# Two-layer spectral and cosine convolution on one core: the row sums of layer 1 are issued one step later

## The chip, the cores and the metric

The kernel runs on one core of a Trainium2 chip. The metric is the device time of one execution in microseconds (us). Five engines work side by side, each through a queue of its own, in order: PE (matrix multiplications; PEld is its weight load), DVE (VectorE), ACT (ScalarE), POOL (GpSimd) and SP, which here only issues DMAs. An engine whose next instruction waits for another engine does nothing else meanwhile.

## The reference

The input `x` is 4 images of 512 x 512 pixels with 16 channels, in float32. Each of two layers adds a convolution of the group-normalised input to the input. Layer 0 is a long convolution in the frequency domain; its code is left out here, since the change is in layer 1:

```python
def _L1_conv_ref(x, kernel, bias, radius):
    ones_f = jnp.ones((K, K, C, 1), dtype=x.dtype)          # K = 3, C = 16
    input_norm = jnp.sqrt(lax.conv_general_dilated(x * x, ones_f, strides, 'SAME', dimension_numbers=DN) + EPS)
    kernel_norm = jnp.sqrt(jnp.sum(kernel * kernel, axis=(0, 1, 2), keepdims=True) + EPS)
    y = lax.conv_general_dilated(x, kernel / kernel_norm, strides, 'SAME', dimension_numbers=DN)
    y = y / input_norm
    y = 1.0 - jnp.arccos(y) * (2.0 / jnp.pi)
    y = y * (jnp.tanh(kernel_norm / radius) * jnp.tanh(input_norm / radius))
    return y + bias
...
x = x + _L0_conv_ref(_gn(x), L0_conv_h0, L0_conv_numerators, L0_conv_denumerator)
x = x + _L1_conv_ref(_gn(x), L1_conv_kernel, L1_conv_bias, L1_conv_radius)
```

So every output pixel needs, beside its 3 x 3 convolution, the sum of squares of the 3 x 3 x 16 inputs around it, of which the kernel takes the root, the reciprocal and the hyperbolic tangent.

## The kernel before

The kernel has four phases, one after the other: the filter of layer 0, the forward transform, the product in the frequency domain, and `last_phase`, which transforms back (until about 14,740 us in the profile) and then computes layer 1. Only layer 1, the last 1,750 us, is touched.

**Units and groups.** Layer 1 cuts the four images into 64 groups; a group is 32 columns of one image over all its 512 rows. A group `g` has four units `u = 4g ... 4g+3`, each of 128 rows x 32 columns x 16 channels, and also four blocks `q = 4g ... 4g+3`, each of 8 columns over all rows. For a unit or a block there are these pieces of work (the lines are those of the profile):

- `block(q)`: PE transposes the input (`pt`, L1183), ACT normalises it (`xn`, L1191) and squares it (`x2`, L1193).
- `squares(q)`: PE sums the squares over channels (four matmuls, `p2`, L1209, into a PSUM tile of one buffer), DVE copies the sums to `e_sum` (L1213). The sums of a group need one column of each neighbour, which POOL copies: at `k == 0` into the group before (L1215), at `k == 3` into the group after (L1218).
- `over_w(g)`: POOL adds the three neighbouring columns (two additions, L1222 and L1223, into `e_sum3`; the profile calls it `e_sum`).
- `norms(g)`: PE adds the three neighbouring rows (three matmuls into `pn`, L1230 to L1232), ACT takes the root (`l_inn`, L1237) and, once for two groups, in the odd one, the tanh (`l_th`, L1239), DVE the reciprocal (`l_rin`, L1241). It issues no DMA.
- `border(g)`: POOL gathers the columns beside a group (L1259), PE transposes them (L1262), DVE normalises them (`e_bn`, three instructions, L1271).
- `conv(u)`: PE, twelve matmuls of the 3 x 3 convolution (L1279) and one of the border (L1287), into one of four PSUM tiles `pc`.
- `cosine(u)`: DVE, `pc` times `l_rin` (`e_y`, L1297). `root` and `factors`: seven instructions of ACT (L1303 to L1315). `gate` and `signed`: two of POOL (L1320, L1325), the first of which reads `l_th`. `chain(u)`: DVE, three products (L1331), one more (L1332), and `e_o` (L1334), after which the tile `pc` is free again. `finish(u)`: POOL adds the input (L1339), SP stores the result (L1341).

Beside that, `prepare()` makes the next image ready until about 15,760 us: POOL adds (`p_x`, L1071), DVE takes statistics (L1067), SP loads and stores.

**What sets the order.** A loop calls `step(u)`, and `step` calls the pieces above, each for a unit or group ahead of or behind `u` (`lead` is 14). In `step` the sums of group `g` and the norms of group `g` come from two lines:

```python
g, k = divmod(u + lead - 3 - 4, 4)
if k == 0 and 0 <= g < n_groups:
    norms(g)
...
g, k = divmod(u + lead - 2 - 4, 4)
if k == 0 and 0 <= g < n_groups:
    over_w(g)
```

The first lies near the start of `step`, before `block` and `conv`; the second at its end. So `over_w(g)` is issued at the end of step `4g-8`, and `norms(g)` near the start of the next one, `4g-7`, just after `squares(4g+6)`. The order in which the instructions then stand in the queues is not this order of calls: a scheduler of the framework places each instruction on its engine, from the order of the calls, the dependencies and the buffers. A change of one call can therefore move other instructions too, on every engine.

Of the kernel before, what the change touches and what calls it, by code (L numbers as in the profile page):

```python
# [961 lines left out]
def last_phase(tc, cst, x, y_d, yw_d, t_d, kern, bias, radius, out):  # L962
    nc = tc.nc
    with ExitStack() as ctx:
# [206 lines left out]
        def load(g):  # L1171
            t = xp.tile([P, 4, 32, C], F32, name="xt")
            b, wt, w = order[g // 16], g % 16 // 4, g % 4 * 32
            nc.sync.dma_start(
                out=t, in_=t_d[b][wt].rearrange("(h p) w c -> p h w c", p=P)[:, :, w : w + 32, :]
            )
            xt[g] = t

        def block(q):

            pt = ps_t.tile([P, N], F32, name="pt")
            for h in range(4):
                nc.tensor.transpose(  # L1183
                    pt[:, h * P : (h + 1) * P],
                    xt[q // 4][:, h, q % 4 * 8 : q % 4 * 8 + 8, :].rearrange("p w c -> p (w c)"),
                    ident,
                )
            xn = np_.tile([P, N + 2], F32, name="xn")
            nc.gpsimd.memset(xn[:, 0 : N + 2 : N + 1], 0.0)
            vec = vecs[order[q // 64]]  # L1190
            nc.scalar.activation(xn[:, 1 : N + 1], pt, AF.Identity, scale=vec[:, 0:1], bias=vec[:, 1:2])  # L1191
            x2 = ew.tile([P, N], F32, name="x2")
            nc.scalar.activation(x2, xn[:, 1 : N + 1], AF.Square)  # L1193
            xns[q], x2s[q] = xn, x2
# [9 lines left out]
        def squares(q):  # L1204

            g, k = q // 4, q % 4
            p2 = ps_s.tile([P, 4, 8], F32, name="p2", tag="gn_ps")
            for h in range(4):
                nc.tensor.matmul(p2[:, h], x2s[q][:, h * P : (h + 1) * P], cols, start=True, stop=True)  # L1209
            del x2s[q]  # L1210
            if g not in sums:
                edges(g)
            nc.vector.tensor_copy(sums[g][:, :, 1 + 8 * k : 9 + 8 * k], p2)  # L1213
            if k == 0 and g % 16 > 0:
                nc.gpsimd.tensor_copy(sums[g - 1][:, :, 33:34], sums[g][:, :, 1:2])  # L1215
            if k == 3 and g % 16 < 15:
                edges(g + 1)
                nc.gpsimd.tensor_copy(sums[g + 1][:, :, 0:1], sums[g][:, :, 32:33])  # L1218
# [7 lines left out]
        def norms(g):  # L1226

            s3 = st["s3"]
            pn = ps_n.tile([P, 4, 32], F32, name="pn")
            nc.tensor.matmul(pn, over_h[:, 0], s3, start=True, stop=False)  # L1230
            nc.tensor.matmul(pn[:, 1:4], over_h[:, 1], s3[:, 0:3], start=False, stop=False)
            nc.tensor.matmul(pn[:, 0:3], over_h[:, 2], s3[:, 1:4], start=False, stop=True)  # L1232
            if g % 2 == 0:
                st["inn"] = ew.tile([P, 2, 4, 32], F32, name="l_inn")
                st["th"] = ew.tile([P, 2, 4, 32], F32, name="l_th", bufs=4)
            inn, th = st["inn"], st["th"]
            nc.scalar.activation(inn[:, g % 2], pn, AF.Sqrt, bias=eps1)  # L1237
            if g % 2:
                nc.scalar.activation(th, inn, AF.Tanh, scale=rrad)  # L1239
            rin = ew.tile([P, 4, 32], F32, name="l_rin", bufs=4)  # L1240
            nc.vector.reciprocal(rin, inn[:, g % 2])  # L1241
            rins[g], ths[g] = rin, th[:, g % 2]
# [9 lines left out]
        def border(g):  # L1252

            t = ew.tile([P, 4, 3, 2, C], F32, name="e_bx")
            for side in range(2):
                at, w = (g + 2 * side - 1, 31 - 31 * side)
                if at // 16 != g // 16 or at < 0:
                    at, w = g, 0
                nc.gpsimd.tensor_copy(t[:, :, :, side], bc(xt[at][:, :, w, :], 2, [P, 4, 3, C]))  # L1259
            pt = ps_t.tile([P, N], F32, name="pt")  # L1260
            for h in range(4):
                nc.tensor.transpose(pt[:96, h * P : (h + 1) * P],  # L1262
                                    t[:, h].rearrange("p d s c -> p (d s c)"), ident)
            bx = ew.tile([96, N], F32, name="e_bn")
            nc.gpsimd.memset(bx[0:32, 0:1], 0.0)
            nc.gpsimd.memset(bx[64:96, N - 1 : N], 0.0)
            vec = vecs[order[g // 16]]
            for dh in range(3):
                r = slice(32 * dh, 32 * dh + 32)
                lo, hi = max(1 - dh, 0), min(N + 1 - dh, N)  # L1270
                nc.vector.tensor_scalar(bx[r, lo:hi], pt[r, lo + dh - 1 : hi + dh - 1],  # L1271
                                        vec[r, 0:1], vec[r, 1:2], ALU.mult, ALU.add)
            borders[g] = bx

        def conv(u):
            h, ts = u % 4, list(terms(u // 4))
            pc = ps_c.tile(sh, F32, name="pc")
            for n, (q, dh, lo, hi, o) in enumerate(ts):
                nc.tensor.matmul(  # L1279
                    pc[:, lo:hi, :].rearrange("p w j -> p (w j)"),  # L1280
                    xns[q][:, h * P + dh : h * P + dh + P],
                    bands[dh][:, o : o + hi - lo, :].rearrange("p w j -> p (w j)"),
                    start=(n == 0), stop=False,
                )

            lo, hi = int(u // 4 % 16 == 0), 2 - int(u // 4 % 16 == 15)
            nc.tensor.matmul(  # L1287
                pc[:, 31 * lo : 31 * hi - 30 : 31, :],
                borders[u // 4][:, h * P : (h + 1) * P], eband[:, lo:hi], start=False, stop=True,
            )  # L1290
            if h == 3:
                del borders[u // 4]
            pcs[u] = pc

        def cosine(u):
            y = ew.tile(sh, F32, name="e_y", bufs=4)
            nc.vector.tensor_mul(y, pcs[u], bc(rins[u // 4][:, u % 4, :], 2, sh))  # L1297
            st["y", u] = y

        def root(u):  # L1300

            v = ew.tile(sh, F32, name="e_v", bufs=3)
            nc.scalar.activation(v, st["y", u], AF.Abs)  # L1303
            nc.scalar.activation(v, v, AF.Relu, scale=-1.0, bias=1.0)
            nc.scalar.activation(pcs[u], v, AF.Sqrt, scale=ARC[7] ** 2)  # L1305
            st["v", u] = v
# [11 lines left out]
        def gate(u):  # L1318
            t = ew.tile(sh, F32, name="e_gate")
            nc.gpsimd.tensor_mul(t, bc(ths[u // 4][:, u % 4, :], 2, sh), bc(ktn, 1, sh))  # L1320
            st["gate", u] = t

        def signed(u):
            t = st["gate", u]
            nc.gpsimd.tensor_mul(t, t, st.pop(("y", u)))  # L1325
# [11 lines left out]
        def finish(u):  # L1337
            g, h, o = u // 4, u % 4, st.pop(("o", u))
            nc.gpsimd.tensor_add(o, o, xt[g][:, h])  # L1339
            w = g % 16 * 32  # L1340
            nc.sync.dma_start(out=out[order[g // 16], h * P : (h + 1) * P, w : w + 32, :], in_=o)  # L1341

        lead = 14

        def step(u):
            if u % 4 == 0 and (u + lead) // 4 + 2 < n_groups:
                load((u + lead) // 4 + 2)
            if 0 <= u + lead - 1 < n_units:
                squares(u + lead - 1)

            g, k = divmod(u + lead - 3 - 4, 4)
            if k == 0 and 0 <= g < n_groups:
                norms(g)
            if u + lead < n_units:
                block(u + lead)
            if u % 4 == 2 and 0 <= u + 6 < n_units:
                border((u + 6) // 4)
            if 0 <= u + 3 < n_units:
                conv(u + 3)
            if 0 <= u < n_units:  # L1360
                signed(u)
            if 0 <= u - 1 < n_units:
                finish(u - 1)
            if 0 <= u + 1 < n_units:
                root(u + 1)
                gate(u + 1)
                factors(u + 1)
            if 0 <= u < n_units:
                chain(u)
            if 0 <= u + 2 < n_units:  # L1370
                cosine(u + 2)
# [3 lines that stand above are left out]
            if u >= 0:  # L1375
                next(beside, None)
            for q in [q for q in xns if q < u]:
                del xns[q]
# [5 lines left out]
        for u in range(-lead, n_units + 1):  # L1384
            step(u)
# [50 lines left out]
```

## Time and profile before

| what | us |
|---|---|
| median of 3 runs | 16473.95 |
| lowest and highest of them | 16464.4 and 16498.5 |
| the profiled execution, its own time | 16489.29 |
| its span in the profile | 16487.4 |
| layer 1 within it (from about 14,740) | 1,750 |
| PE's waits for `over_w` within it (60 of the 64 groups) | 135.7 |

The profile comes from one execution, which lies 15 us above the median; 2 us of it lie outside the span. Lines of a timeline give the start, the duration, the engine, the line, the operation, what is written and read, and in square brackets how long the engine was idle before it and what ended the wait. A matmul of float32 data is shown as two records on PE, so the twelve of a `conv` are counted as 24; the four transposes of a `block` are counted as 4.

### The profile page before, as it was taken

To read this page: it belongs to the slowest core of one execution; us is meant where nothing else is said; L and a number is where in the kernel's file an instruction comes from. 1 tells how busy PE (TensorE), PEld (TensorE's weight loads), DVE (VectorE), ACT (ScalarE), POOL (GpSimd) and SP (SyncE) were. 2 spreads that over 40 slices of the span, in tenths; PEclk is the share of its full clock that TensorE was granted. 3 is DMA by queue.
4 is the path that set the end of the run, shared out by engine and by line. 5 is a ranking of instruction groups with operands and counts; after the bars stand their busy time and mean duration, and the time that the engine had idled before them with its cause. 6 is when DMAs were issued, how large, how long until landed. Compare 5 with 4: busy or idle time off the path is not lost. (4 is left out here: it accounts for less than half of the span.)

```text
span 16487.4 us, 538106 instructions
## 1 busy us (share of the span) xinstructions
PE 15039.9 (91%) x232588; PEld 11221.5 (68%) x232588; DVE 10549.6 (64%) x20763; ACT 8870.6 (54%) x17007; POOL 10203.4 (62%) x9645
## 2 busy tenths in 40 slices
PE   7999999999988889898988899888889998988898
PEld 5555555554567777677777777777777777777787
DVE  8999999974545555555555555555555552447877
ACT  4666666653345555555555555555555551027888
POOL 7777777763356666666666666666666660237766
PEclk8999999999999999999999999999999999989999
DMA  4888888888888888888888888888888886885531
GB/s 139 241 244 247 240 243 248 240 244 250 251 282 328 324 326 330 317 327 329 328 329 317 326 328 327 317 318 324 324 326 329 326 321 232 313 279 167 167 110 67
DMA packets 2914640, 4542.92 MB, mean 276 GB/s; under 512 B 126114, under 2 KB 2094460, under 8 KB 2801422
## 3 DMA queue, kind: packets, MB, share of 16 engines
q1 hardware_dynamic: 2703070, 3836.37, 67.9%
q0 software_dynamic: 172336, 605.00, 9.5%
q10 hardware_dynamic: 36864, 67.13, 1.2%
q8 instruction: 1833, 30.03, 0.7%
q14 instruction: 537, 4.40, 0.1%
HBM read 3030.71 MB, written 1477.31 MB: 273 GB/s over the span
## 5 line engine op out<-in xcount | busy, mean ns | idle before, releaser
L828 PE MATMUL pg<-c_dg,g 64*128 64x128 f32 x32832 | 2838.7, 290 | 344.4 <-ACT gh L728 192.2
L844 PE MATMUL pm<-xe,gh 128*32 128x64 f32 x131328 | 2380.2, 222 | 520.0 <-issue 299.3
L844 PEld LDWEIGHTS pm<-xe,gh 128*32 128x32 f32 x131328 | 2001.1, 110 | 1113.6 <-issue 891.7
L828 PEld LDWEIGHTS pg<-c_dg,g 64*128 64x128 f32 x32832 | 2277.5, 189 | 690.3 <-issue 248.1
L873 DVE TENSOR_TENSOR z<-zq,pz 128x256 f32<-128x256 f32 x2052 | 859.5, 419 | 2634.6 <-ACT zq L872 2567.4
L726 DVE COPY gh<-pg 128x512 f32<-128x512 f32 x2046 | 1408.2, 688 | 1208.9 <-PE pg L828 1205.8
L458 PE MATMUL pt<-ev_in,c_todd 128*128 128x512 f32 x4096 | 1927.5, 609 | 16.2 <-DMA ev_in<-g_d 16.2
L797 POOL TENSOR_TENSOR xu<-xe,c_late 128x256 f32<-128x256 f32 x2052 | 1391.7, 702 | 808.5 <-ACT xe L728 791.2
L388 DVE RECIPROCAL dn<-dn 128x256 f32<-128x256 f32 x1024 | 1722.8, 1724 | 17.6
L728 ACT COPY yf<-pm 128x512 f32<-128x512 f32 x2046 | 1211.4, 592 | 886.9 <-PE pm L844 873.2
L389 POOL TENSOR_TENSOR sp<-m,dn 128x512 f32<-128x512 f32 x1024 | 1300.9, 1271 | 592.4 <-DVE dn L388 552.0
L808 ACT COPY xe<-xl 64x1024 f32<-64x1024 f32 x513 | 538.7, 1050 | 1877.9 <-POOL xl L799 1877.8
L728 ACT COPY gh<-pg 128x512 f32<-128x512 f32 x2058 | 1200.2, 583 | 368.8 <-PE pg L828 365.7
L865 PE MATMUL pz<-c_ident,yf 128*128 128x128 f32 x8208 | 1371.7, 290 | 24.2 <-issue 10.8
L458 PEld LDWEIGHTS pt<-ev_in,c_todd 128*128 128x128 f32 x4096 | 728.2, 190 | 920.6 <-issue 792.3
L417 ACT COPY st<-pg 128x256 f32<-128x256 f32 x2048 | 616.8, 391 | 1301.5 <-PE pg L406 1301.3
L406 PEld LDWEIGHTS pg<-c_dinv,sp 64*128 64x128 f32 x16384 | 1005.5, 196 | 442.2 <-ACT sp L394 232.6
L799 POOL TENSOR_TENSOR xl<-xl,xu 128x1024 f32<-128x1024 f32 x513 | 1209.5, 2358 | 40.2
L406 PE MATMUL pg<-c_dinv,sp 64*128 64x128 f32 x16384 | 1108.2, 287 | 60.2 <-ACT sp L394 44.6
L881 POOL TENSOR_TENSOR zd<-z 128x512 f32<-128x512 f32 x513 | 653.7, 1274 | 765.4 <-DVE z L873 765.3
L1279 PE MATMUL pc<-l_band,xn 128*128 128x160 f32 (+2 forms) x6144 | 1076.2, 333 | 51.7 <-DVE e_o L1334 51.7
L913 POOL DMA_DIRECT2D y_d<-yo x511 | 296.5, 580 | 1325.0 <-ACT yo L728 1299.8
(211 smaller groups left out, 30193.2 us busy)
## 6 DMA issues: line engine op xcount, KB each, us to landing
xe<-xf_d SPq DMA_DIRECT2D x1026, 1536.0 KB
g<-g_d SPq DMA_DIRECT2D x511, 1024.0 KB
g_d<-st SPq DMA_DIRECT2D x256, 1024.0 KB
ev_in<-g_d SPq DMA_DIRECT2D x1024, 256.0 KB
g_d<-ot SPq DMA_DIRECT2D x1024, 256.0 KB
xf_d<-xe POOLq DMA_DIRECT2D x513, 448.0 KB, 8.2
xf_d<-xl POOLq DMA_DIRECT2D x513, 448.0 KB, 5.4
x_d<-xo SPq DMA_DIRECT2D x128, 1024.0 KB
```

What stands on the lines that cost most here:

```text
L388: nc.vector.reciprocal(dn, dn)
L389: nc.gpsimd.tensor_mul(w["sp"][:, v], w["m"][:, v], bc(dn, 2, [P, 2, 2, P]))
L406: nc.tensor.matmul(pg[u][:, n, k].rearrange("p a x -> p (a x)"), w["sp"][q, n, k, c, :], dinv[q, 2 * kp + k, c, :], start=(c == 0), stop=( ...
L458: nc.tensor.matmul(pt, todd[:, c, kc, hh * P : hh * P + P], ev[:, kc, c], start=(kc == 0), stop=(kc == 1),)
L726: nc.vector.tensor_copy(dst, src)
L728: nc.scalar.copy(dst, src)
L797: nc.gpsimd.tensor_mul(u[:, :, h, c], xe[:, :, h, 1 - c], bc(late[:, 1 + c], 2, [P, F, 2]))
L799: nc.gpsimd.tensor_add(xl.rearrange("p f h c k -> p (f h c k)"), xl.rearrange("p f h c k -> p (f h c k)"), u.rearrange("p f h c k -> p (f ...
L828: nc.tensor.matmul(pg[c][:, j % 4], g[half, j], dg[half], start=True, stop=True)
L844: nc.tensor.matmul(pm[32 * q : 32 * q + 32, g % 8], gh[:, f].rearrange("p c j -> p (c j)"), xe[:, :, f].rearrange("p t h c k -> p t (h c k ...
L865: nc.tensor.transpose(pz[:, t % 4].rearrange("p v q x -> p (v q x)"), y[:, at].rearrange("p g x -> p (g x)"), ident)
L1279: nc.tensor.matmul(pc[:, lo:hi, :].rearrange("p w j -> p (w j)"), xns[q][:, h * P + dh : h * P + dh + P], bands[dh][:, o : o + hi - lo, :] ...
```

## The change

`norms(g)` moves from step `4g-7` to step `4g-6`. Its place within the step, just after `squares` and before `block`, stays, and so does the place of `over_w(g)` at the end of step `4g-8`. Nothing is added or removed; the instructions and their operands are the same.

```diff
@@ -1348,7 +1348,7 @@
             if 0 <= u + lead - 1 < n_units:
                 squares(u + lead - 1)
 
-            g, k = divmod(u + lead - 3 - 4, 4)
+            g, k = divmod(u + lead - 8, 4)
             if k == 0 and 0 <= g < n_groups:
                 norms(g)
             if u + lead < n_units:
```

## The prediction

> **What bounds the kernel now.** I first cut layer 1 into stretches by the busy time of each engine. Here is one stretch while the next image is still prepared, and one after; the columns are PE, PEld, DVE, ACT, POOL and PE's granted clock.
>
> ```profile
> core 0: us, PE busy (x) PEld busy (x) DVE busy (x) ACT busy (x) POOL busy (x), PEclk, DMA share, GB/s
> 15100.00:15300.00 200.00, 171.97 (x1166) 151.49 (x1165) 165.87 (x334) 163.95 (x284) 149.28 (x183) 0.93 0.50 165
> ...
> 16100.00:16300.00 200.00, 180.87 (x1228) 159.60 (x1228) 151.77 (x249) 169.80 (x292) 125.83 (x183) 0.95 0.22 77
> ```
>
> PE leads with 86% and 90%, but ACT and DVE are close: whatever PE gains, they must be able to follow. DMA is half used. Next, who waits for whom, from 15,200 to 16,300 us (total, times, longest):
>
> ```profile
> PE pn L1230 <- POOL e_sum L1223: 78.5, 41, 7.9
> PE pc L1279 <- DVE e_o L1334: 31.9, 45, 3.0
> ACT l_inn L1237 <- PE pn L1232: 7.1, 3, 3.7
> POOL p_x L1071 <- DMA p_x<-in_x: 5.1, 4, 3.3
> ```
>
> Most of PE's idle time ends with `over_w`, on which the first norms matmul waits; in all of layer 1 it is 135.7 us in 60 groups. The second wait is for a free `pc`: a conv can start when DVE's `e_o` four units back is done. How the two look in time, after preparation has ended:
>
> ```profile
> 16202.21 1.04 PE L1209 MATMUL p<-c_cols,x 128*128 128x8 f32 x8
> 16204.15 3.98 PE L1279 MATMUL pc<-l_band,xn 128*128 128x512 f32 x24 [0.90 <-DVE e_o L1334]
> ...
> 16214.00 1.04 PE L1209 MATMUL p<-c_cols,x 128*128 128x8 f32 x8
> 16214.89 1.07 PE L1183 MATMUL pt<-c_ident,xt 128*128 128x128 f32 x8
> 16217.68 0.80 PE L1230 MATMUL pn<-e_sum,c_over_h 128*128 128x128 f32 x2 [1.72 <-POOL e_sum L1223]
> ```
>
> The norms come right behind the squares that they need (here with two blocks of transposes between), so PE sits out the chain copy (DVE) - copy (POOL) - two additions (POOL). A last look, while the image is prepared, at the longest kind:
>
> ```profile
> 14906.67 2.85 POOL L1071 TENSOR_TENSOR p_x<-p_x,p_y 128x1024 f32<-128x1024 f32 x1 [5.11 <-DMA p_x<-in_x]
> 14910.83 2.84 POOL L1071 TENSOR_TENSOR p_x<-p_x,p_y 128x1024 f32<-128x1024 f32 x1
> 14914.59 0.80 PE L1230 MATMUL pn<-e_sum,c_over_h 128*128 128x128 f32 x2 [9.84 <-POOL e_sum L1223]
> ```
>
> POOL, in order, waits for a load and works 2 x 2.85 us on the next image, with `over_w` behind it; PE waits 9.84 us.
>
> **What the Trainium skill says.** "Perfetto Trace Analysis", Optimization Strategy: a gap that repeats on the engine that should be saturated can mean too few SBUF or PSUM buffers. The 0.90 us gap is of that kind (four `pc` tiles); the 1.72 us one is a plain dependency. "TensorE: Matmul & The Clock Gate", What's actually happening: the PE clock is halved after an idle window of about 3.4 us, and the window runs free. The trace agrees in direction: a conv whose 24 matmuls take 3.82 us otherwise takes 4.2 to 6.0 after norms waits of over 2.5 us; after 1.5 to 1.7 us it is sometimes 3.7, sometimes 4.5 to 5.5. "ScalarE: Activation LUTs", What ACT_TABLE_LOAD costs: 1283 ns a load; the trace has 1283, and the built order still has one tanh per pair of groups, so I count no more loads.
>
> **The change part by part.** No instruction is added; I compare the built orders of both versions.
>
> *Norms on PE.* Only 22 of 64 groups get them later. Counted from a group's first block, five squares stood ahead of its norms before (its own four and the neighbour's one that it needs); now it is eight (groups 5, 7, 9, 11, 17, 19, 21, 23, 25, 29, 33), seven (35, 45, 49, 51, 53, 55, 57, 59, 61) or six (13, 41). They are all odd. The even groups keep their place directly behind the squares, so they keep their waits (1.3 to 1.6 us mostly). Taking the wait of each of the 22 from the timeline: 44.6 us in the eleven, 16.6 in the nine, 12.1 + 0.6 in the two: **-73.9 us**. In these groups the matmuls of the next conv took 13.7 us beyond 3.82 each: **-13.7 us**, if the waits caused it.
>
> *POOL.* Before those odd norms POOL has only come one `finish` further, PE two or three convs. So `over_w` is one to three units (about 6 us each) ahead; these waits go whole, the long ones too unless something else takes them up.
>
> *Root on ACT.* It now stands one unit (5.1 us of work) later, and in odd groups PE reaches its norms after conv `4g-4` rather than `4g-7`. ACT may stand idle for it: from the same block's transposes ACT works 5.1 us to the root, PE 6.3 (conv 3.9, squares 0.9, norms 0.75, rest), so about 1.3 us a pair of groups. ACT waits more than that for PE's transposes already (60.8 us from 15,960 to 16,400); I count zero. Behind the root wait the next block's normalising and squaring, which PE's squares need only after another conv. The tanh is one unit nearer its first `gate`, with two left; zero.
>
> *DVE, where the cost is.* The reciprocal (0.86 us pitch) moves one unit, and the scheduler repacked the queue around it. A conv needs, after the squares before it, DVE's `e_sum` copy, then what stands up to `e_o`. In the example above that is copy 0.1 + `e_o` 0.75 = 0.90 with nothing of PE's between, 0.42 with a border's transposes. Late (nine pairs, groups 44 to 61) the new queue has, once a pair, copy - L1332 - `e_y` - `e_o`, and once copy - L1332 - reciprocal - `e_o`. PE has one block's transposes (0.48) to cover it: 0.1 + 0.6 + 0.6 + 0.75 + 0.1 (from engine to engine) - 0.48 = 1.7, and with 0.86 for the reciprocal 1.9. That makes 3.6 a pair for 0.90 + 0.42 = 1.3 before: 9 x 2.3 = **+20.7 us**. Behind the waiting conv stand its squares and the next transposes, for which ACT then waits. While the image is prepared (15 pairs, 4 to 33) the copy is followed by L1332 and an `e_bn` (0.8), 1.8 us for 0.4, and the eight L1067 in a row (0.29 each) delay another `e_o` by some 0.6: 15 x 2.0 = **+30 us**, an estimate from these durations.
>
> *SP.* Norms move past no DMA, but loads and stores are repacked. POOL's waits for the load of `p_x` are 22.9 us in layer 1, in 10 times; bounds: that much less, or that much more. I take the middle, zero.
>
> Sum: -73.9 - 13.7 + 20.7 + 30 = **-36.9 us**, from the profiled 16489.3 to 16452.4; the median of the runs is 15.3 lower, so **16437**. Two runs of before differ by up to 34 us, so I take 0.2% (33 us) as what can be told from no change.
>
> **The rivals.**
>
> *The full gain* (part of faster). DVE uses its slack (17 to 24%) and no wait replaces the old one: -87.6, 16386. For it: DVE waits for squares often (70.5 us from 15,960 to 16,400). Against: those waits are what ties `e_o` to the squares.
>
> *It moves to `pc` and little is left* (same). Of the 73.9 us, 48.8 lie in six groups with waits over 4.9 us, where POOL stood behind a late load. The same POOL delay also holds `signed`, hence `e_o`, hence a conv; and now pairs of L1071 stand directly ahead of the copy for even groups. If half of it comes back: -36.9 + 24.4 = -12.5, 16461.
>
> *Slower*. In the 24 pairs, DVE's place ahead of `e_o` costs two stalls of 1.7 to 1.9 us, longer than the 0.4 to 0.9 of before, with even norms' 1.5 close by. From about 1.7 us the conv after may run slow: if each costs 1.5 more, 2 x 24 x 1.5 = +72, and with 25 coming back by POOL the sum is -36.9 + 72 + 25 = +60, 16534. It decides against the change from about 40 slow convs more than before. For it: conv bursts of 5.2 to 6.8 us after waits for `e_o` of 2.9 us; against: 3.82 after one of 1.64.
>
> That *the change does not do what it says* is half true: in 42 groups the norms don't stand later on PE.
>
> **How the numbers follow.** The forecast and the full gain together are faster: 0.50 (0.36 and 0.14). Same: 0.28. Slower: 0.22, for a repacked queue on four engines that are all 75 to 90% busy has more ways to lose than I have priced. The range leaves a tenth at each end: from 16375, a little beyond the full gain, with POOL's load waits gone too, to 16515, into the slower case.
>
> **What would show it.** In the changed profile: waits of L1230 for L1223 at some 60 us instead of 135.7, none in groups 45 to 61 odd; waits of L1279 for `e_o` up by about 50 us over layer 1, in steps near 1.7 and 1.9; conv bursts over 4.2 us not more than before. The forecast is wrong if L1230 still waits over 100 us, if L1279's waits take back over 70, or if the span moves outside layer 1.

## The result, and the profile after

The changed kernel takes 16449.4 us (median of 14 runs, 16425.6 to 16497.1), the kernel before 16475.4 us (14 runs beside them): a ratio of 0.9986 with a 95% interval of 0.9978 to 0.9994. That is 26 us faster, a small gain but one that the interval tells from nothing. It is smaller than the 33 us that the prediction had set as what can be told from no change. The forecast was 16437 us, the range 16375 to 16515.

The profiled execution of the changed kernel took 16433.1 us with a span of 16431.3. "Layer 1" is from here on the time from the first transpose of L1183 to the end of the span: 1769.1 us before, 1729.5 after, **39.6 us less**. The other 16.5 us between the two spans lie ahead of it, in phases that the change does not touch. They are taken as chance here: in the nine profiles with the preparation beside layer 1, its start lies anywhere between 14694.6 and 14727.9 us.

First the two stretches of layer 1, in the columns of the prediction (PE, PEld, DVE, ACT, POOL, granted clock of PE):

```profile
15100.00:15300.00 200.00, 183.37 (x1234) 161.61 (x1233) 175.89 (x356) 172.23 (x294) 148.05 (x191) 0.94 0.50 165
16100.00:16300.00 200.00, 182.02 (x1192) 161.15 (x1191) 144.51 (x236) 164.75 (x280) 120.30 (x176) 0.91 0.19 70
```

While the images are prepared, every one of these engines gets through more instructions in 200 us than before (1234 matmul records instead of 1166). After that it is the other way round: PE is busier (182.0 us instead of 180.9) and does *less* (1192 records instead of 1228), at a clock of 0.91 instead of 0.95. The waits of PE from 15,200 to 16,300 us (total, times, longest):

```profile
PE pc L1279 <- DVE e_o L1334: 45.2, 44, 2.0
PE pn L1230 <- POOL e_sum L1223: 37.2, 23, 4.6
PE pt L1183 <- DVE e_bn L1271: 9.1, 5, 1.8
```

The wait of the norms for `over_w` has halved (78.5 before), that of the convs for `e_o` has grown by 13 us, and that of the transposes for `e_bn`, one wait of 4.1 us before, is now 9.1 us in five. The timeline of an odd group, number 5, whose norms waited 4.96 us before:

```profile
14848.21 1.04 PE L1209 MATMUL p<-c_cols,x 128*128 128x8 f32 x8
14849.11 0.47 PE L1230 MATMUL pn<-e_sum,c_over_h 128*128 128x128 f32 x2
```

No bracket: no wait. The sums of this group had left POOL at 14838.1, 11 us earlier. And a late stretch, where the prediction put its two stalls (a stall is a wait of PE in the middle of its work):

```profile
16131.23 0.63 PE L1183 MATMUL pt<-c_ident,xt 128*128 128x128 f32 x4
16133.46 5.66 PE L1279 MATMUL pc<-l_band,xn 128*128 128x512 f32 x24 [1.59 <-DVE e_o L1334]
...
16140.44 3.88 PE L1279 MATMUL pc<-l_band,xn 128*128 128x512 f32 x24
...
16147.67 5.66 PE L1279 MATMUL pc<-l_band,xn 128*128 128x512 f32 x24 [1.84 <-DVE e_o L1334]
```

The stalls are there, with 1.59 and 1.84 us (1.7 and 1.9 were worked out). DVE's queue in the first of them is the one of the prediction:

```profile
16131.42 0.19 DVE L1213 COPY e_sum<-p 128x32 f32<-128x32 f32 x1 [3.77 <-PE p L1209]
16131.52 0.69 DVE L1332 SCALAR_TENSOR_TENSOR pc<-e_v,pc 128x512 f32<-128x512 f32 x1
16132.12 0.69 DVE L1297 TENSOR_TENSOR e_y<-pc,l_rin 128x512 f32<-128x512 f32 x1
16132.72 0.68 DVE L1334 SCALAR_TENSOR_TENSOR e_o<-pc,e_gate 128x512 f32<-128x512 f32 x1
```

What the sum did not have is the second column of the PE lines: a conv behind such a stall takes 5.66 us, the one between them 3.88. The two slow convs cost 2 x 1.67 us (5.49 to 3.82, from the start of the conv to that of the next instruction), and that is the whole loss of the late part: a pair of groups without these slow convs takes 51.3 us, most late pairs of the changed kernel 54.7. The granted clock of PE (the third number from the right) over these three convs is:

```profile
16133.46:16138.95 5.49, 5.49 (x25) 4.92 (x25) 3.32 (x5) 5.49 (x11) 2.57 (x5) 0.69 0.58 206
16140.44:16144.16 3.72, 3.72 (x27) 3.24 (x26) 3.62 (x6) 3.72 (x8) 3.72 (x6) 1.00 0.18 70
16147.67:16153.17 5.50, 5.50 (x25) 4.53 (x26) 3.82 (x6) 4.33 (x8) 4.83 (x4) 0.69 0.13 51
```

These are means over a conv: the record behind them has the clock at half of full speed in a part of each slow conv, and full in the whole of the other. This holds for all convs of layer 1: in the profile of the changed kernel each of the 52 over 4.2 us has such a part of more than 0.7 us, and no other conv has.

Where the 39.6 us lie, by the start of the norms of a group (one profiled execution of each; groups 44 to 46 and the two ends, some -4 us together, are left out):

| stretch | before | after | difference |
|---|---|---|---|
| groups 0 to 4 | 77.8 | 83.6 | +5.8 |
| groups 4 to 34, images being prepared | 840.4 | 796.1 | **-44.3** |
| groups 34 to 44 | 270.3 | 257.2 | -13.1 |
| groups 46 to 62, per pair of groups | 52.1 | 54.15 | **+2.05** |

So the change wins beside the preparation and loses behind it. The experiments ask whether that is so, and whether the loss is the stall or the clock.

### The profile page after: what moved, and what is told of

The parts are those of the page before. It is cut to its first block, busy times and chain, and to the rows that moved or that the text cites. A ratio compares the mean times of both kernels' runs of the same rounds, so it can differ in the third digit from the quotient of the medians.

```text
span 16431.3 us, 538072 instructions
## 1 busy us (share of the span) xinstructions
PE 15026.8 (91%) x232588; PEld 11215.8 (68%) x232588; DVE 10547.2 (64%) x20763; ACT 8868.5 (54%) x17007; POOL 10205.4 (62%) x9645
```

## The experiments

Every time is given as a ratio to runs of the kernel before on the same chip, since these moved between 16474 and 16489 us from one set to the next. "Layer 1", "groups 4 to 34" and "late pair" (the mean of the eight pairs from group 46 to 62) are us of one profiled execution each; the last column counts the convs that took over 4.2 us from their start to that of the next instruction. "Preparation ahead" means that the next images are all made ready before layer 1 begins. "Fillers" are matmuls whose results nobody reads, put where PE would wait. In the kernels with fillers the lines of the squares and of their copy stand one further down (L1210, L1214), the fillers are L1217, and what follows stands four further down: L1283 is the conv, L1234 the norms, L1338 `e_o`.

| kernel | median us | ratio (95%) | layer 1 | groups 4 to 34 | late pair | convs over 4.2 us |
|---|---|---|---|---|---|---|
| before | 16475 | 1 | 1769.1 | 840.4 | 52.1 | 39 |
| changed | 16449 | 0.9986 (0.9978 to 0.9994) | 1729.5 | 796.1 | 54.15 | 52 |
| e1, later for groups 0 to 43 alone | 16437 | 0.9965 (0.9952 to 0.9977) | 1720.9 | 796.0 | 51.7 | 39 |
| e2, before, preparation ahead | 16768 | 1.0168 (1.0154 to 1.0182) | 1681.3 | 778.0 | 51.7 | 36 |
| e3, changed, preparation ahead | 16821 | 1.0197 (1.0183 to 1.0211) | 1729.0 | 796.6 | 53.3 | 70 |
| e4, norms of older sums | 16407 | 0.9948 (0.9934 to 0.9962) | 1684.5 | 777.9 | 51.6 | 36 |
| e5, changed, fillers late | 16423 | 0.9972 (0.9962 to 0.9982) | 1711.8 | 799.7 | 51.0 | 35 |
| e6, e3 with fillers | 16723 | 1.0159 (1.0143 to 1.0174) | 1667.8 | 765.7 | 51.2 | 30 |
| e7, e3 with the copy on ACT | 16802 | 1.0203 (1.0190 to 1.0217) | 1743.7 | 789.8 | 54.6 | 54 |
| e8, later for even groups alone | 16468 | 0.9997 (0.9989 to 1.0006) | 1769.5 | 827.5 | 52.5 | 53 |
| e9, changed, fillers everywhere | 16437 | 0.9968 (0.9955 to 0.9980) | 1721.5 | 799.3 | 50.9 | 27 |
| e10, e9 and fillers in the even norms' wait | 16412 | **0.9958** (0.9945 to 0.9972) | 1695.1 | 795.6 | 49.3 | 14 |
| e11, before, fillers in the norms' wait | 16434 | 0.9974 (0.9964 to 0.9984) | 1721.7 | 826.1 | 49.85 | 17 |

### Which part of layer 1 gains: e1, e2, e3

e1 takes the later place for the first 44 groups and the earlier one for the rest:

```diff
-            g, k = divmod(u + lead - 8, 4)
-            if k == 0 and 0 <= g < n_groups:
-                norms(g)
+            for off, part in ((8, range(44)), (7, range(44, n_groups))):
+                g, k = divmod(u + lead - off, 4)
+                if k == 0 and g in part:
+                    norms(g)
```

> The step later only for groups 0 to 43 (the groups beside the preparation of the next images), the earlier place for groups 44 to 63. Theory: the gain lies beside the preparation and is partly given back after it, because the queue of DVE then ties e_o to the squares twice a pair, with waits of 1.6 and 1.8 us on PE and slow convs behind them. Then this kernel keeps the gain and drops the loss: some 15 us faster than the changed kernel, 40 us faster than the one before (about 16435), and a late pair of groups takes 51.5 us as before, not 54.7. Rival: the late loss of the one profiled execution is not of the change; then the time is that of the changed kernel (16449) or, as it has fewer groups moved, nearer the one before, and late pairs take 53 us or more here too.

The theory held in its direction: 0.9965 against 0.9986 for the change as a whole. How much it is stays rough: the ratios differ by 0.0021 or 35 us, the medians by 12, layer 1 in the profiles by 9 (15 were expected). Late pairs take 51.7 us, and the stretch of groups 4 to 34 has the 796 us of the changed kernel to the tenth. In the traces the four computing engines run that stretch in the changed kernel's order, but for one DVE instruction, so the late loss belongs to the late order and can be left out.

e2 and e3 are the kernel before and the changed kernel with one addition each:

```diff
         while order[0] not in vecs:
             next(beside)
+        for _ in beside:
+            pass
         for g in range(3):
             load(g)
```

> The kernel before, with the preparation of the images finished ahead of layer 1, so that POOL, DVE and the queues have nothing of it beside layer 1. To be compared with the same for the changed kernel. Theory: POOL's long detours, and with them the norms waits of over 2.5 us, are gone; every pair of groups takes 51 to 52 us as the late pairs of the kernel before do, and the waits of L1230 for over_w are 32 x 3 = some 80 us or less in sum. Layer 1 alone takes about 1680 us instead of 1769; the whole is slower by what the preparation takes by itself.

> The changed kernel, with the preparation finished ahead of layer 1 in the same way. Theory: the gain of the change comes from the waits that the preparation makes, so without it the step later costs: a pair takes 54 to 55 us, some 30 x 3.2 = 95 us more than in the kernel before with the preparation ahead (0.5 to 0.6 %). If the slow convs of the late part were chance, 30 x 0.2 = about 0. Rival, the gain has nothing to do with the preparation (a norms wait less in every second group): 30 to 40 us faster than the other one.

e2 came as expected in layer 1 (1681.3 us), though its norms still wait 91.7 us and not 80 or less. With nothing of the preparation beside it, the change is a loss, and e3's rival is out: 16821 us against 16768, 52 us, in the same set of runs and with intervals that do not touch. The 95 us of the theory were too many, for not every stall is followed by a slow conv. The layers by themselves, in the columns of the windows above (e2 first, then e3; each stretch begins with its layer 1):

```profile
15085.00:16767.00 1682.00, 1509.64 (x10372) 1337.80 (x10372) 1262.25 (x2091) 1437.89 (x2465) 1043.51 (x1516) 0.95 0.23 82
```

```profile
15090.00:16820.00 1730.00, 1555.51 (x10372) 1381.31 (x10372) 1265.88 (x2092) 1444.92 (x2465) 1047.95 (x1516) 0.92 0.23 79
```

PE has the same 10372 records in both and is busy 45.9 us longer in e3; the layer is 47.6 us longer. PE's idle time, added up from its gaps, is 157.1 and 158.8 us. So the difference is the clock, 0.92 against 0.95. The waits did only change their name, here e2 and then e3 over layer 1:

```profile
PE pn L1230 <- POOL e_sum L1223: 91.7, 58, 1.7
PE pc L1279 <- DVE e_o L1334: 48.6, 67, 3.0
```

```profile
PE pc L1279 <- DVE e_o L1334: 98.8, 61, 2.9
PE pn L1230 <- POOL e_sum L1223: 49.0, 34, 1.5
```

42.7 us went from the norms and 50.2 came to the convs. In e3, 55 convs stand behind a stall of 1.58 to 1.85 us: 35 of them take 5.25 to 5.5 us from start to start, one takes 6.76, 19 take 3.82, and there is nothing between.

### What the norms' wait is worth at most: e4

The norms of a group use the sums of the group before, so the right sums are left out of the result, and PE hardly ever waits for `over_w`:

```diff
-            st["s3"] = s3
+            st["s3"], st["old"] = s3, st.get("s3", s3)
...
-            s3 = st["s3"]
+            s3 = st["old"]
```

> The kernel before, in which the norms of a group read the column sums of the group before it, which have long been there; the sums that belong to the group are still worked out but not used by its norms, so that part of the computation is left out. The orders of all queues stay as before; only PE does not wait for over_w. It gives the full price of the norms wait. Theory: 135.7 us of waits and part of the 57 us of slow convs go, and waits of the convs for e_o (51.7 us) stay about as they are, since DVE's queue is unchanged: 16475 - 150 = about 16325. Rival, DVE and ACT have no room: the waits move to L1279 for e_o and to L1183 for e_bn, these grow by 70 us or more, and the time is 16400 to 16440.

The rival won. The wait is gone (135.7 us to 2.9), and the layer is shorter by 84.6 us, not by 150. The waits of PE over layer 1:

```profile
PE pc L1279 <- DVE e_o L1334: 113.1, 89, 3.3
PE pt L1183 <- ACT xn L1191: 14.9, 27, 2.0
...
PE pn L1230 <- POOL e_sum L1223: 2.9, 3, 1.9
```

61.4 us came back at `e_o` and 14 more at the transposes, and 36 convs are still slow. So 132.8 us of norms waits gone brought 84.6 us: 54.0 less idle time of PE and 30.5 less busy time at a better clock. This is not the wait's worth alone, for the queues did not stay as before, though the expectation said so: of the 1388 instructions of DVE in groups 4 to 34, 97 stand in another order than in the kernel before, and 9 of 512 in the late part.

### The stall or the clock: e5 and e6

The fillers are four matmuls behind the squares ahead of each of the two stalls. They write spare columns of the squares' own PSUM tile, and PE runs them in 1.16 us:

```diff
-            p2 = ps_s.tile([P, 4, 8], F32, name="p2", tag="gn_ps")
+            pw = ps_s.tile([P, 160], F32, name="p2", tag="gn_ps")
+            p2 = pw[:, 0:32].rearrange("p (h w) -> p h w", h=4)
...
+            if q >= 176 and q % 8 in (5, 7):
+                for _ in range(4):
+                    nc.tensor.matmul(pw[:, 32:160], over_h[:, 0], ident, start=True, stop=True)
```

> The changed kernel, with four 128x128 matmuls of no use behind the squares of those blocks whose copy holds e_o up in the late part (block 5 and 7 of eight, from block 176 on); they write spare columns of the squares' PSUM tile. They stand on PE where it would sit still for 1.6 and 1.8 us. Theory: the loss of the late part is not the waits (4.96 us a pair against 4.8) but the slow clock after them; with PE at work in the wait the conv after it takes 3.82 us again instead of 5.5, late pairs take some 51.4 us instead of 54.7, and the whole 25 to 30 us less than the changed kernel, about 16423. Rival, the convs behind these waits are slow for another reason (they wait for data in steps): no change, or slower by the added 18 x 0.3.

> The changed kernel with the preparation ahead of layer 1, and the same useless matmuls from block 20 on, so in all pairs of groups. Theory: of the 52 us by which the changed kernel with the preparation ahead is slower than the one before with it ahead, the slow clock is nearly all: convs over 4.2 us fall from 70 to about 36, and the time from 16820 to about 16770. Rival: the waits for e_o themselves are the loss (98.8 us against 48.6); then it stays at 16820 or grows.

Both go by the theory, e6 further than it. In the traces the four computing engines run the late part of e5 in the order of the changed kernel, fillers apart, and all of groups 4 to 34 and 46 to 62 of e6 in that of e3, but for at most two instructions of an engine. So these two pairs differ by the fillers alone. e5 takes 16423 us, as expected; its last seven pairs take 51.3 us each. In e6 every pair from group 6 on takes 51.2 or 51.3 us, but for three of 50.6, where e3 has a mixture of 51.3 and 54.7. Layer 1 is 61.2 us shorter than in e3 (the ratio falls by 0.0038, which is 63 us), and even 13.5 us shorter than in e2. Here is one stall of e6, which in the changed kernel would be 1.6 us long:

```profile
16135.39 1.04 PE L1210 MATMUL p<-c_cols,x 128*128 128x8 f32 x8
16136.71 1.16 PE L1217 MATMUL p<-c_ident,c_over_h 128*128 128x128 f32 x8 [0.28 <-DVE e_sum L1214]
16137.70 0.60 PE L1183 MATMUL pt<-c_ident,xt 128*128 128x128 f32 x4
16138.50 3.98 PE L1283 MATMUL pc<-l_band,xn 128*128 128x512 f32 x24 [0.20 <-DVE e_o L1338]
```

The conv starts no earlier in relation to its squares, 3.1 us after they began, as in the changed kernel; but it takes 3.98 us and not 5.66. What was lost is therefore neither the stall nor late data, but the clock behind the stall. Over the 60 places with fillers layer 1 gains about 1.0 us each: 1.67 us where the clock would have been lost, nothing where it would not (36 x 1.67 is 60).

### Another way round the tie: e7 and e8

e7 takes `e_sum`'s copy off DVE, in the kernel of e3:

```diff
-            nc.vector.tensor_copy(sums[g][:, :, 1 + 8 * k : 9 + 8 * k], p2)
+            nc.scalar.copy(sums[g][:, :, 1 + 8 * k : 9 + 8 * k], p2)
```

> The changed kernel with the preparation ahead of layer 1, and the copy of the squares' sums moved from DVE to ACT, so that DVE's e_o no longer stands behind an instruction that waits for PE's squares. Theory: the tie of e_o to the squares is that copy; the waits of L1279 for e_o fall from 98.8 us to under 50, slow convs with them, and the time from 16820 to some 16750. Rival: ACT, in order too, is tied to the squares instead and its normalising comes late, so that PE waits at L1183 or L1209 for ACT, 50 us or more: 16800 to 16850.

The ratio is that of e3 within the intervals. The waits for `e_o` fell only to 68.0 us, in fewer and longer ones (20 of 2.3 to 2.4 us), and 26.4 us came at L1183 for ACT's `xn`: the rival's move of the tie to ACT, half as large as it said. That the copy on DVE alone is the tie is refuted. There are fewer slow convs, 54 instead of 70, but 26 of them now take 6.2 to 6.8 us, and together they lose more (119.0 us beyond 3.82 each, and 96.7 in e3).

e8 moves only the even groups:

```diff
-            g, k = divmod(u + lead - 8, 4)
-            if k == 0 and 0 <= g < n_groups:
-                norms(g)
+            for off, par in ((8, 0), (7, 1)):
+                g, k = divmod(u + lead - off, 4)
+                if k == 0 and 0 <= g < n_groups and g % 2 == par:
+                    norms(g)
```

> The step later only for even groups. In the built order it is then again the odd groups whose norms stand seven or eight squares behind their first block, and DVE has the run copy, L1332, reciprocal, e_o once a pair, but not the run copy, L1332, e_y, e_o. Theory, the loss is in these runs: the gain beside the preparation stays and a late pair takes 51.4 to 53 us: 16425 to 16440. Rival, any norms a step later costs the same late: 16449 as the changed kernel.

Neither was right. Late pairs do take 52.5 us, within the theory's range, but the gain beside the preparation is not there: norms wait 102.1 us, 53 convs are slow, and the total is the kernel before's. The order of the late part did not foretell the rest, and why the norms wait so long here is not shown.

### How far the clock carries: e9, e10, e11

The fillers of e5, from block 20 on (e9); also behind block 4 of eight, in the wait of the even norms (e10); and the kernel before with fillers in the norms' wait of every group (e11). The condition of e5's edit becomes:

```diff
-            if q >= 176 and q % 8 in (5, 7):
+            if q >= 20 and q % 8 in (5, 7):       # e9
+            if q >= 20 and q % 8 in (4, 5, 7):    # e10
+            if q >= 20 and q % 4 == 0:            # e11, with norms(g) in the place of before
```

> The changed kernel, preparation beside layer 1 as ever, with the useless matmuls behind the squares of block 5 and 7 of eight from block 20 on, not only from 176. Theory: while the next images are prepared the order brings stalls of the same kind, but mixed with waits for POOL of many lengths, so that only part of them is filled: the 27 us of the late part and some 20 more of the 38 us by which the convs before it are too long, 16400 to 16410. Rival: the fillers stand in the way where nothing was idle (some 26 of them at 1.16 us in those pairs): 16425 or more.

> As the last, and with the same fillers behind block 4 of eight, where PE sits still for 1.5 us ahead of the norms of the even groups. Theory: that wait too costs more by the slow clock behind it than by itself; late pairs go from 51.3 to 50 to 50.5 us, and the whole to 16385 to 16400. Rival: the slow clock there has no room to cost more, since late pairs already have their 51.3 us, and the fillers are work in the way: no gain over the last, or a loss of up to 30 x 1.16.

> The kernel before, with the same fillers behind the first block's squares of every group from group 5 on, so in the norms wait of every group. It tells what part of the norms wait's price in the kernel before was the clock, and whether the change still gains when both have fillers. Theory: of the 57 us by which its convs are too long some 25 go, and nothing of the 135.7 us of waits: about 16450, 40 to 50 us more than the changed kernel with its fillers. Rival: with the clock held up the two orders are equal within 15 us.

e9 brings nothing over e5, and its rival was right: 16437 us, where the theory had 16400 to 16410. While the images are prepared its slow convs are fewer (27 in all), but the norms wait 87.8 us instead of 69.8, and the stretch of groups 4 to 34 stays at 799 us. That stretch is 796 to 800 us in five kernels with the later norms, with fillers or without. What sets it there no run shows: in e9 and e10 the scheduler also reordered it (some 185 of 1380 instructions of DVE), so that these two do not test the fillers alone there. In the late part they do, but for at most three instructions of DVE, ACT or POOL and 18 of 2592 records of PE. e10 is faster than both kernels, with intervals that do not touch, and has the lowest median of those that leave nothing out; the intervals of e1, e5, e9 and e11 overlap with its own. The 16385 to 16400 us of its theory were not reached (16412), but its late pairs take 49.3 us, less than the 50 to 50.5 expected, and PE has its full clock there:

```profile
16100.00:16300.00 200.00, 193.57 (x1412) 175.33 (x1411) 159.32 (x260) 182.45 (x312) 132.52 (x197) 1.00 0.19 70
```

So the 51.3 us of a late pair were no floor; the 1.5 us waits ahead of the even norms cost their clock too. e11 says the same of the kernel before: fillers alone, without the change, make it 0.9974, by the ratio more than the change brings by itself, though the two intervals overlap. The theory had 16450 us for it and underrated the clock. Its clock in the same window is 1.00 as well, and its late pairs take 49.85 us, so with the clock held up the changed order no longer loses in the late part. With fillers in both, the changed order is still ahead, by 22 us of the medians and 26.6 us in layer 1, between the 40 to 50 of the theory and the 15 of the rival. The two intervals overlap, though, so this rests on one profiled execution of each more than on the medians.

## Why the prediction was right, point by point

The forecast, 36.9 us less, stands beside 39.6 us less in the profiled layer 1 and 26 us between the medians. The median lies midway between the forecast (16437) and the rival "it moves to `pc` and little is left" (16461), so the total does not decide between them. The place does: that rival wanted POOL's delay to come back at `e_o`, and in groups 4 to 34 the waits for `e_o` grew by 2.1 us only. Of the terms:

- **Norms on PE, -73.9.** In the 22 groups this came exactly: 73.9 us of waits before, none after. But the other 42 groups, put at no change, went from 61.9 to 69.8 us, above all group 3, which now waits 9.3 us, and group 4 with 6.3 (0.6 and 1.9 before). All norms waits are 69.8 us, where "some 60" was written. Of the odd groups 45 to 61 one, 47, waits 0.8 us.
- **Slow convs behind norms, -13.7.** In the convs right behind the 22 norms this came too: 13.7 us beyond 3.82 each before, nothing after. What failed is what the sum put at nothing beside it, slow convs behind other waits. The time beyond 3.82 us of all convs grew from 57.3 to 75.9, so some 32 us came at other convs; convs over 4.2 us went from 39 to 52, where "not more than before" was written. The prediction had that mechanism, with 1.5 us a time, but put it into the rival "slower" alone; 1.67 us, in most of the 17 slow convs behind 21 stalls of this kind in the changed kernel, belonged into the sum. Over all that PE does, busy time in layer 1 fell by 4.0 us (1551.40 to 1547.45), since squares and norms took some 19 us less.
- **Late, +20.7.** Stall lengths were right to 0.1 us. Waits for `e_o` in the late part rose from 12.0 to 25.6 us (over eight pairs), +13.6; but 11.2 us less of norms waits stand against them, so that idle time in a late pair is 4.8 us in both kernels. The waits were nearly right, then. The eight pairs are 16.4 us longer all the same, and what makes them longer is the clock.
- **While the images are prepared, +30.** This was mis-sized: waits for `e_o` in groups 4 to 34 went from 26.2 to 28.3 us. In their stead the transposes of L1183 wait 14.5 us for `e_bn`, eight times up to 1.8, a wait of DVE's queue that was not foreseen. The term is some 17 instead of 30. Over all of layer 1 the waits for `e_o` grew by 15.8 us, where "about 50" was written.
- **POOL, ACT and SP at nothing.** PE's waits for `xn` at the transposes rose from 0.5 to 2.0 us, and POOL's for the load of `p_x` fell from 22.9 to 16.7; zero was near enough.

In sum, PE's idle time in layer 1 fell by 35.6 us (202.8 to 167.2), where the terms for it make 23.2, and its busy time by 4.0, where 13.7 stood. The two errors have opposite signs and nearly cancel. So the direction, the place and the waits of the 22 groups were foreseen, but that the sum lies within 3 us of the profile is luck.

The rival "slower" did not decide, for it took 1.5 us for 48 convs, and the convs over 4.2 us are 13 more, not 40; but e3, where nothing beside layer 1 gives the longer waits that the change removes, is that rival: slower, by its mechanism. Of the signs of being wrong one came up: the span moved outside layer 1 too. By the spread of layer 1's start, given above, those 16.5 us tell nothing of the change.

"TensorE: Matmul & The Clock Gate" of the Trainium skill, What's actually happening, gives two clock states with a ratio of two and a free-running window of about 3.4 us. The traces agree: their record of the granted clock knows full and half speed alone, and in each of the 13 profiles every change between them in layer 1 falls on one raster of 3.413 us. In e3 69 of the 71 stretches at half speed last one step of it. The price measured here agrees as well: half speed for 3.4 us costs 1.7 us of work, as an estimate from those two figures, and most slow convs behind a stall cost 1.67. Its section HAM oscillation names gaps over about 3.4 us as what to avoid. That does not carry over: stalls of 1.5 to 1.85 us, with the squares and transposes around them, were enough here.

Why they are enough no experiment tested, but the traces point to the small matmuls. Take each step of the raster at full speed in layer 1 and count PE's busy time in it without the squares. Over the 13 profiles it is under half a step (1.71 us) in 503 of the 516 steps that half speed follows, and in 132 of the 5177 that full speed follows; in e3 alone in 69 of 70 and 5 of 355. With the squares counted, no limit parts the steps so well (in e3 15 fall on the wrong side at best). So the eight records of the squares, 1.04 us, seem to count for little. The limit was chosen after the fact and is not tested.

## What to carry to other kernels

Price a stall of PE with the clock that it can lose behind it: here 1.6 us of waiting cost 1.67 us more or nothing, and two orders with the same idle time differed by 46 us. When an order is changed to remove a wait, ask not only how long the new waits are but whether they are longer each than the old; if they can't be removed, work of no use in them may pay. A placing that helps beside other work can cost without it, so try it only for the steps where that work runs, as e1 does.

## What was not expected of the hardware

- Four useless 128x128 matmuls (1.16 us) in a stall of 1.6 us shorten the conv behind it from 5.5 to 3.82 us; in 60 places they save 61 us of layer 1 (e6 against e3).
- The loss of clock comes in fixed portions: of 55 convs behind stalls of 1.58 to 1.85 us (e3) 35 lost 1.4 to 1.7 us, one lost 2.9 and 19 lost nothing. In e7, behind stalls of 2.15 to 2.4 us, 21 of 23 lost two portions: 6.7 to 6.8 us instead of 3.82. Behind norms waits of 1.5 us the portion is spread over transposes, norms and the conv (0.91 us for four transposes instead of 0.63, then 4.94 for a conv).
- With every regular late wait of 1.5 us and more filled, the granted clock was 1.00 over 200 us (e10 and e11), where the kernel before had 0.95 and the changed one 0.91.
